# A gated graph network and a graph attention layer on one core: eight unread matrix products, a product and a spread moved in TensorE's last stage, and one subtraction moved behind a copy at the start

## The chip, the core and the metric

The kernel runs on one NeuronCore of a Trainium2 chip. Its engines are TensorE (PE in the profile; its weight loads are PEld), VectorE (DVE), ScalarE (ACT), GpSimd (POOL) and the sync engine (SP), which issues most transfers. Each engine works through its own queue in order and waits on semaphores for the others. The metric is the device time of one execution in microseconds; lower is better.

## The reference

64 graphs of 256 nodes with 256 features, an integer adjacency matrix each. Two layers, both with a layer norm and a ReLU ahead and a residual behind:

```python
# layer 0: gated graph network, 3 steps
h = relu(layernorm(x))
A = (adj != 0)
for i in range(3):
    m = h @ weight[i]
    aggr = einsum('bst,bsd->btd', A, m)
    h = gru_cell(aggr, h, w_ih, w_hh, b_ih, b_hh)
x = x + h

# layer 1: graph attention, 4 heads of 64
h = relu(layernorm(x))
f = h @ W.T + b                               # values, per head
logits = leaky_relu(f·a_src [row] + f·a_dst [column], 0.2)
logits = where(adj == 1, logits, -9e15)
out = softmax(logits) @ f
x = x + out
```

## The kernel before

The graphs are worked two at a time: 32 pairs, numbered 0 to 31, of 512 rows each. A pair passes through three recurrent steps (class `Step`, six ticks each) and then through the attention stage. Work of several pairs is interleaved: `at(tick, phase, p, fn)` puts each piece of work into a plan, and at the end the plan is read out tick by tick. What is read out is recorded in that order, and each engine gets its instructions in that order; nothing is reordered afterwards. PSUM has eight banks, in two pools: five for the gates (`gate_bank`) and three for the rest (`bank`). A new tile takes a bank of its pool when the last reader of the tile before it has finished, so the order of the work also decides who waits for a bank.

**The start.** For pair 0, `xn` is the normalised input (L368, VectorE). `first_hi` (L834, ScalarE) rounds its ReLU to the high halves `hNhi`, and `first_lo` (L838, VectorE) subtracts to get the low halves `hNlo`. At about the same place of the plan, `step_weights(0, [3])` multiplies weights on TensorE (`pc`, L243) and copies the two results to SBUF, the first on VectorE and the second on ScalarE (L247). The transposes `pt_a` (L387) and `pw_hh` (L182) follow on TensorE, in the same three banks; VectorE copies the first two `pw_hh` to `hh_T` (L183) and makes `edge` from the adjacency (L818); then the first aggregation `pa` (L493) begins. The plan has `rest(-3 if p else -6, first_lo)` for `first_lo`, `at(-6, REST, 0, ...)` for `step_weights(0, [3])`, and the biases at -5.

**The end.** For the last pair (31) `plan_tail` writes out one list, `order`, by hand, in which the rest of pairs 29 and 30 is laid between the steps of pair 31. In the code, `do(what, 2, ...)` is work of pair 29 and `do(what, 1, ...)` of pair 30. The pair's two graphs are told apart by an index 0 or 1. The steps that matter here:

- `g.difference`, `g.update` (L577, L582, L583, VectorE): the end of the last recurrent step; their result is `hT_a`.
- `turn_back` (`pback`, TensorE) transposes it back, `residual` (VectorE) adds it to `x`, `stats` and `result` (L642 to L655, VectorE, with a power on POOL, L646) normalise to `xn_b`, `turned` (`pt_b`, L664, TensorE) transposes that, with a ReLU on ScalarE (L667) to `hT_b`.
- `values` (`pv`, L673, TensorE) and `values_out` (L680, VectorE) make the values `val`.
- `spread_neighbours` (`drow`), `spread_own` and `own_and_link` (`own`), and `spread_tops` (`mrow`) spread scores over all partitions by transposes on TensorE (L688, L714, L720). `link` holds the mask as bf16 numbers, written well before.
- `maxima` (L747 to L754, VectorE) finds the row maxima `top`; `logits` and `leaky` build the logits; `exps` adds `mrow` on VectorE (L763) and takes the exponential on ScalarE (L764; for pair 30, L1040).
- `product` and `out` (`po`, L597, TensorE) multiply with the values, 16 matmul records each; `divided` divides on VectorE (`rden` L606, `o` L612) or ScalarE (L610) and adds to `x` on POOL or VectorE (L617); `write` stores to DRAM from SP's queue (L586).

The rows of pair 30's maxima are added to its logits by two transfers of 1 MB that POOL issues (`add_rows`, L986).

Of the kernel before, what the change touches and what calls it, by code (L numbers as in the profile page):

```python
# [27 lines left out]
def gated_gnn_then_gat_kernel(  # L28
# [39 lines left out]
    nc = tc.nc  # L68
# [29 lines left out]
    def bank(name):  # L98
        return ps_m.tile([P, 512], F32, tag="mm", name=name)
# [5 lines left out]
    def buf(tag, shape, name, dtype=F32):  # L105
        return sb.tile(shape, dtype, tag=tag, name=name, bufs=BUFS.get(tag, 1))
# [50 lines left out]
    ident16 = const.tile([P, P], BF16, name="ident16")  # L157
    nc.vector.tensor_copy(ident16, ident)

    def gate_bank(name):  # L160
        return ps_g.tile([P, 512], F32, tag="g", name=name)
# [460 lines left out]
    def plan_tail(t0, p, v, g, turn_back, residual):  # L622
# [15 lines left out]
        def stats(i):  # L638
            st = small.tile([P, KN, 6], F32, tag="st", name=f"st_b{p}_{i}")
            mv[i] = small.tile([P, KN, 2], F32, tag="mv", name=f"mv_b{p}_{i}")  # L640
            for s in range(KN):
                nc.vector.bn_stats(st[:, s, :], v["x"][:, i * KN + s, :])  # L642
                nc.vector.bn_aggr(mv[i][:, s, :], st[:, s, :])
            rstd[i] = small.tile([P, KN], F32, tag="rstd", name=f"rstd_b{p}_{i}")
            nc.vector.tensor_scalar_add(rstd[i], mv[i][:, :, 1], EPS)
            nc.gpsimd.tensor_tensor(rstd[i], rstd[i], mhalf[:, :KN], ALU.pow)  # L646

        def result(i):
            if i == 0:
                v["xn"] = buf("xn", [P, R, D], f"xn_b{p}")  # L650
                v["hT_b"] = buf("hT_b", [P, KD, T], f"hT_b{p}")
                v["val"] = buf("val", [P, R, VW], f"val_{p}")
                v["top"] = small.tile([P, R, H], F32, tag="top", name=f"top_{p}", bufs=2)
            for s in range(KN):
                nc.vector.tensor_scalar(  # L655
                    v["xn"][:, i * KN + s, :], v["x"][:, i * KN + s, :], mv[i][:, s, 0:1], rstd[i][:, s : s + 1],
                    op0=ALU.subtract, op1=ALU.mult,
                )

        def turned(i):  # L660
            pt = bank(f"pt_b{p}_{i}")
            for k in range(KD):
                for s in range(KN):
                    nc.tensor.transpose(  # L664
                        pt[:, k * N + s * P : k * N + (s + 1) * P], v["xn"][:, i * KN + s, ts(k, P)], ident
                    )
            nc.scalar.activation(of(v["hT_b"], i), by_c(pt), AF.Relu)  # L667

        def values(i):
            for r in range(i * KN, (i + 1) * KN):  # L670
                pv[r] = bank(f"pv_{p}_{r}")
                for k in range(KD):
                    nc.tensor.matmul(  # L673
                        pv[r][:, :VW], v["hT_b"][:, k, ts(r, P)], w_val[:, k, :],
                        start=(k == 0), stop=(k == KD - 1),
                    )

        def values_out(i):
            for r in range(i * KN, (i + 1) * KN):
                nc.vector.tensor_add(v["val"][:, r, :], pv[r][:, :VW], b_val)  # L680
# [62 lines left out]
        def maxima(i):  # L743
            for h_ in range(H):
                for r in range(i * KN, (i + 1) * KN):
                    any_ = buf("any", [P, N], f"any_{p}_{r}_{h_}")
                    nc.vector.tensor_tensor_reduce(  # L747
                        any_, two(drow[i][h_ // 2])[:, h_ % 2, :], v["noedge"][:, r, :], 1.0, -3.0e38,
                        ALU.add, ALU.max, accum_out=v["top"][:, r, h_ : h_ + 1],
                    )  # L750
            t = v["top"][:, xs[i], :]
            nc.vector.tensor_add(t, t, v["val"][:, xs[i], S0 : S0 + H])
            nc.vector.scalar_tensor_tensor(t, t, ALPHA, t, op0=ALU.mult, op1=ALU.max)
            nc.vector.tensor_scalar(t, t, barred, -1.0, op0=ALU.max, op1=ALU.mult)  # L754

        def spread_tops(i):
            mrow[i] = spread(i, "mrow", v["top"])

        def exps(i):
            for y in range(H // 2):  # L760
                for j in range(KN):
                    z_ = pairs_of_heads(i, j)[y]
                    nc.vector.tensor_add(z_, z_, two(mrow[i][y]))  # L763
                    nc.scalar.activation(z_, z_, AF.Exp)  # L764

        def out(r):
            product(p, r, zz[r // KN], v, gate_bank)

        def do(what, q, *key):
            return left[what, p - q, *key]  # L770

# [1 line left out]
        order = (  # L773
            lambda: g.difference(0), lambda: g.update(0), do("product", 2, 0), do("rows", 1), do("product", 2, 1),
            lambda: turn_back(0), lambda: g.difference(1), lambda: residual(0), lambda: stats(0), lambda: g.update(1),
            do("add", 1), do("product", 2, 2), lambda: turn_back(1), lambda: result(0), lambda: turned(0),
            lambda: residual(1), lambda: stats(1), do("product", 2, 3), do("divided", 2, 0), lambda: values(0),
            lambda: result(1), do("divided", 2, 1), lambda: turned(1), lambda: values_out(0), do("divided", 2, 2),
            do("divided", 2, 3), do("write", 2), lambda: spread_neighbours(0), lambda: own_and_link(0, 0),
            lambda: leaky(0, 0, psum=True), lambda: values(1), lambda: own_and_link(0, 1),  # L780
            lambda: leaky(0, 1, psum=True), lambda: maxima(0), lambda: values_out(1), lambda: spread_tops(0),
            lambda: spread_own(1), do("exps", 1, 0), do("product", 1, 0), lambda: exps(0),
            lambda: spread_neighbours(1), lambda: logits(1), lambda: leaky(1, 0, 1), do("divided", 1, 0),
            do("exps", 1, 1), lambda: out(0), do("product", 1, 1), lambda: out(1), do("product", 1, 2),
            lambda: maxima(1), lambda: spread_tops(1), do("product", 1, 3), lambda: exps(1),
            lambda: divided(p, 0, v, nc.gpsimd.tensor_add), do("divided", 1, 1),
            lambda: divided(p, 1, v, nc.gpsimd.tensor_add), lambda: write(p, v["x"], 0, KN), do("divided", 1, 2),
            do("divided", 1, 3), do("write", 1),
# [6 lines left out]
    def plan_pair(p):  # L795
        t0 = APART * p
        v = {}
# [9 lines left out]
        def rest(t, fn):  # L807
            at(t0 + t, REST, p, fn)
# [30 lines left out]


        ready(-3 if p else -6.5, first_hi)
        rest(-3 if p else -6, first_lo)

        def back(l, i):

# [13 lines left out]
        def turn_back(l, i):  # L859
            pt = v["pback", i] = bank(f"pback_{p}_{l}_{i}")  # L860
            for s in range(KN):
                for k in range(KD):
                    nc.tensor.transpose(  # L863
                        pt[:, s * D + k * P : s * D + (k + 1) * P], h["hT"][:, k, ts(i * KN + s, P)], ident
                    )

        def residual(i):
            xi = flat(v["x"][:, i * KN : (i + 1) * KN, :])
            nc.vector.tensor_add(xi, v["pback", i], xi)
# [43 lines left out]
        def values(r0):  # L913
            def fn():
                if r0 == 0:
                    v["val"] = buf("val", [P, R, VW], f"val_{p}")
                for r in (r0, r0 + 1):
                    pt = bank(f"pv_{p}_{r}")
                    for k in range(KD):
                        nc.tensor.matmul(  # L920
                            pt[:, :VW], hb["hT"][:, k, ts(r, P)], w_val[:, k, :],
                            start=(k == 0), stop=(k == KD - 1),
                        )
                    if dma_b:
                        nc.vector.scalar_tensor_tensor(
                            v["val"][:, r, :], pt[:, :VW], xn_b["rstd"][:, r : r + 1], b_val,
                            op0=ALU.mult, op1=ALU.add,
                        )
                    else:
                        nc.vector.tensor_add(v["val"][:, r, :], pt[:, :VW], b_val)  # L930
                if r0 == 0:
                    v["score"] = small.tile([P, R, 2 * H], F32, tag="score", name=f"score_{p}", bufs=2)
                nc.vector.tensor_copy(v["score"][:, r0 : r0 + 2, :], v["val"][:, r0 : r0 + 2, S0:])
            return fn
# [64 lines left out]
        def maxima(r, h0):  # L999
            def fn():  # L1000
                if r == 0 and h0 == 0:
                    v["top"] = small.tile([P, R, H], F32, tag="top", name=f"top_{p}", bufs=2)
                for h in (h0, h0 + 1):
                    any_ = buf("any", [P, N], f"any_{p}_{r}_{h}")
                    nc.vector.tensor_tensor_reduce(  # L1005
                        any_, drow[r // KN][:, h, :], v["noedge"][:, r, :], 1.0, -3.0e38, ALU.add, ALU.max,
                        accum_out=v["top"][:, r, h : h + 1],
                    )
            return fn
# [27 lines left out]
        def exps(i, j):  # L1037
            def fn():
                zz = logits[i][:, j, :, :]
                nc.scalar.activation(zz, zz, AF.Exp)  # L1040
            return fn
# [94 lines left out]
```

## Time and profile before

| | |
|---|---|
| median of 3 runs | 2479.35 us (2479.33 to 2479.52) |
| profiled execution | 2477.57 us, of which the span from the first to the last instruction is 2475.7 us |
| PE busy | 2454.0 us (99%) |
| DVE busy | 1983.2 us (80%) |
| ACT busy | 1442.3 us (58%) |
| POOL busy | 495.2 us (20%) |
| mean granted TensorE clock | 0.998 |

All times in the views count from the first instruction of the profiled execution. In a timeline a row is a run of like instructions: start, length, engine, line, operation, output and inputs, shape, number, and in brackets the engine's idle time ahead of it with what ended that. In a table of stretches each engine has its busy time with the number of instructions in brackets, then the granted clock of TensorE (1.00 is full), the busy share of the DMA engines and the rate. The trace's first record of the granted clock stands at 5.07 us; what lies ahead of that is shown as 1.00 for want of a record.

### The profile page before, as it was taken

The numbers are of one execution on the slowest core, as the hardware profiler recorded it, in microseconds if no ns is written. First come the engines' busy times: TensorE is split into PE (matmuls) and PEld (weight loads), VectorE is DVE, ScalarE is ACT, GpSimd is POOL, SyncE is SP. The second block draws the span as 40 slices with busy tenths as digits, with TensorE's granted clock in tenths as the row PEclk, the third lists the DMA queues.
The fourth block names the chain that finished last, engine by engine and source line by source line (L and its number), as shares of the span: only waits on it lengthen the run. The fifth ranks groups of instructions, "written<-read, shape, count | busy, mean of one in ns | idle before, by whom it ended". The sixth has DMA issues, their size and how long they took to land.

```text
span 2475.7 us, 37524 instructions
## 1 busy us (share of the span) xinstructions
PE 2454.0 (99%) x13418; PEld 2184.1 (88%) x13418; DVE 1983.2 (80%) x4659; ACT 1442.3 (58%) x3024; POOL 495.2 (20%) x422
## 2 busy tenths in 40 slices
PE   9999999999999999999999999999999999999998
PEld 7888898888898888888888988888888889888887
DVE  6678887788877888877888778888778887778777
ACT  4455556655556656556555566555565555665666
POOL 0011222112121212121221212121212212121222
PEclk9999999999999999999999999999999999999999
DMA  3026565646656555656456566557564566564455
GB/s 96 26 76 129 129 142 124 157 118 127 145 122 143 138 118 129 154 119 154 115 127 143 131 135 144 116 129 155 115 154 121 126 139 137 129 146 119 102 115 126
DMA packets 322106, 313.72 MB, mean 127 GB/s; under 512 B 166576, under 2 KB 282240, under 8 KB 321920
## 3 DMA queue, kind: packets, MB, share of 16 engines
q0 software_dynamic: 33728, 130.03, 27.8%
q1 hardware_dynamic: 286624, 181.29, 27.7%
q8 instruction: 106, 1.74, 0.3%
q14 instruction: 80, 0.66, 0.1%
q10 hardware_dynamic: 1568, 0.01, 0.0%
HBM read 215.62 MB, written 56.60 MB: 110 GB/s over the span
## 4 chain that ended last, share of the span: by engine, by line
PE 84%; DVE 12%; ACT 3%; issue 1%; DMA 0%; POOL 0%; SPq 0%; ACTq 0%; DVEq 0%; POOLq 0%
PE pd L328 18%; PE pn L328 13%; PE pc L328 10%; PE po L597 9%; PE pe L328 7%; PE pa L493 5%; PE qb L464 5%; PE p L328 5%; PE pv L920 5%; PE qa L464 4%; PE pback L863 2%; DVE hT_a L583 2%; DVE R L582 2%; DVE hNlo L854 1%; DVE any L1005 1%; ACT zz L1025 1%
## 5 line engine op out<-in xcount | busy, mean ns | idle before, releaser
L328 PE MATMUL pn<-aggr,w_a 128*128 128x256 f32 x1536 | 364.9, 380 | 2.8 <-DVE pn L549 2.8
L328 PE MATMUL pd<-T,w_a 128*128 128x256 f32 x1536 | 364.5, 380 | 0.0
L564 POOL TENSOR_TENSOR R<-hT_a,hn 128x512 f32<-128x512 f32 x95 | 140.1, 1475 | 1090.5 <-ACT hn L560 1070.7
L328 PEld LDWEIGHTS pn<-aggr,w_a 128*128 128x128 f32 x1536 | 286.8, 190 | 44.0 <-issue 2.1
L328 PEld LDWEIGHTS pd<-T,w_a 128*128 128x128 f32 x1536 | 286.9, 190 | 37.0
L597 PEld LDWEIGHTS po<-val,zz 128*128 128x128 f32 x2048 | 246.2, 193 | 5.8 <-ACT zz L1040 1.1
L560 ACT ACTIVATE hn<-pn,bi 128x256 f32<-128x256 f32 x384 | 160.8, 471 | 145.8 <-PE pn L328 145.7
L617 POOL TENSOR_TENSOR x<-x,o 128x256 f32<-128x256 f32 x126 | 137.9, 1096 | 538.9 <-DVE o L612 533.8
L582 DVE SCALAR_TENSOR_TENSOR R<-Z,R 128x512 f32<-128x512 f32 x192 | 132.5, 690 | 140.9 <-POOL R L564 126.3
L597 PE MATMUL po<-val,zz 128*128 128x65 f32 x2048 | 243.7, 273 | 0.7 <-ACT zz L1040 0.7
L1025 ACT ACTIVATE zz<-zz,val 128x256 f32<-128x256 f32 x496 | 223.8, 505 | 0.0
L1005 DVE CUSTOM_DVE_ANT_0 any<-drow,noedge 128x256 f32<-128x256 f32 x496 | 208.2, 420 | 10.6 <-DMA drow<-score_dram 1.9
L549 DVE SCALAR_TENSOR_TENSOR pn<-R,hn 128x512 f32<-128x512 f32 x192 | 149.3, 777 | 75.2 <-ACT R L471 53.5
L471 ACT ACTIVATE R<-pc,brz 128x256 f32<-128x256 f32 x192 | 80.6, 471 | 220.8 <-PE pc L328 220.8
L471 ACT ACTIVATE R<-pe,brz 128x256 f32<-128x256 f32 x192 | 80.6, 471 | 213.1 <-PE pe L328 213.1
L328 PE MATMUL pd<-T,w_h 128*128 128x256 f32 x768 | 184.4, 383 | 3.0
L328 PE MATMUL p<-T,w_a 128*128 128x256 f32 x768 | 181.6, 379 | 0.0
L328 PE MATMUL pe<-aggr,w_a 128*128 128x256 f32 x768 | 181.4, 379 | 0.0
L328 PE MATMUL pc<-aggr,w_a 128*128 128x256 f32 x768 | 181.4, 379 | 0.0
L328 PE MATMUL pc<-hT_a,w_h 128*128 128x256 f32 x768 | 181.4, 379 | 0.0
L854 DVE TENSOR_TENSOR hNlo<-pback,hNhi 128x512 fp32r<-128x512 f32 x128 | 88.3, 690 | 114.0 <-ACT hNhi L853 114.0
L328 PEld LDWEIGHTS pd<-T,w_h 128*128 128x128 f32 x768 | 143.5, 190 | 32.7 <-DVE pe L533 14.4
(190 smaller groups left out, 5307.3 us busy)
## 6 DMA issues: line engine op xcount, KB each, us to landing
zz<-score_dram POOLq DMA_DIRECT2D x62, 1024.0 KB, 11.1
zz<-topT_dram POOLq DMA_DIRECT2D x62, 1024.0 KB, 8.0
adj<-in_adj_dram SPq DMA_DIRECT2D x64, 512.0 KB
drow<-score_dram SPq DMA_DIRECT2D x62, 512.0 KB
x<-in_x_dram SPq DMA_DIRECT2D x32, 512.0 KB
out_dram<-x SPq DMA_DIRECT2D x31, 512.0 KB
words_dram_a<-words_a SPq DMA_DIRECT2D x30, 512.0 KB
words_dram_b<-words_b SPq DMA_DIRECT2D x29, 512.0 KB
```

What stands on the lines that cost most here:

```text
L328: nc.tensor.matmul(pt[:, ts(c, N)], w[:, k, j * D + c * P : j * D + (c + 1) * P], src[:, k, :], start=start and c == 0 and k == 0, stop=(c ...
L464: nc.tensor.matmul(pt, w_n[:, j, :], src, start=start, stop=True, skip_group_check=True)
L471: nc.scalar.activation(of(dst, i)[:, c, :], src[:, c, :], AF.Tanh, bias=brz[:, g0 + c : g0 + c + 1], scale=0.5)
L493: nc.tensor.matmul(pt[:, ts(i, N)], hN[half][:, i * KN + s, ts(e, P)], edge[:, i * KN + s, :], start=(s == 0 and half == 0), stop=(s == KN ...
L549: nc.vector.scalar_tensor_tensor(by_c(self.bank(f"pn{i}")), of(self.R, i), 1.0, of(self.hn, i), op0=ALU.add, op1=ALU.mult)
L560: nc.scalar.activation(n__[:, c, :], p_n[:, c, :], AF.Tanh, bias=bi[:, 2 * KD + c : 2 * KD + c + 1])
L564: nc.gpsimd.tensor_sub(of(self.R, i), of(self.hT(), i), n__)
L582: nc.vector.scalar_tensor_tensor(d_, of(self.Z, i), 1.0, d_, op0=ALU.add, op1=ALU.mult)
L597: nc.tensor.matmul(po[:, ts(h_, VC)], zz[:, j, h_, ts(s, P)], v["val"][:, i * KN + j, ts(h_, VC)], start=(j == 0), stop=(j == KN - 1),)
L617: add(v["x"][:, r, :], v["x"][:, r, :], o)
L1005: nc.vector.tensor_tensor_reduce(any_, drow[r // KN][:, h, :], v["noedge"][:, r, :], 1.0, -3.0e38, ALU.add, ALU.max, accum_out=v["top"][:, ...
L1025: nc.scalar.activation(zz[:, h, :], zz[:, h, :], AF.Prelu, alpha=ALPHA, bias=v["val"][:, r, S0 + H + h : S0 + H + h + 1],)
```

## The change

Three edits.

1. In `plan_tail`, a new function `keep` issues four matmuls of `link` (128x512, bf16) with the bf16 identity into a gate bank of its own; nobody reads the result. It stands twice in `order`: behind `turned(0)` and behind `values(0)`. Also, pair 29's fourth product, `do("product", 2, 3)`, goes from behind `stats(1)` to ahead of `turn_back(1)`.
2. In the same list, `maxima(1)` and `spread_tops(1)` go ahead of `do("product", 1, 2)`. Only `spread_tops` and the products are on TensorE's queue; VectorE's own order stays as it was, and so do those of ScalarE, POOL and SP.
3. For pair 0, `first_lo` goes from tick -6 to -5.5. On VectorE's queue the copy of `pc` (L247) then stands ahead of `hNlo` (L838); the other queues keep their order.

The function and the moved entries, cut:

```diff
+        kept = []
+
+        def keep():
+
+            if not kept:
+                kept.append(gate_bank("keep_1"))
+            for _ in range(4):
+                nc.tensor.matmul(
+                    kept[0], ident16, v["link"][:, 0, :, :].rearrange("q j n -> q (j n)"), start=True, stop=True,
+                    skip_group_check=True,
+                )
...
-            do("add", 1), do("product", 2, 2), lambda: turn_back(1), lambda: result(0), lambda: turned(0),
-            lambda: residual(1), lambda: stats(1), do("product", 2, 3), do("divided", 2, 0), lambda: values(0),
-            lambda: result(1), do("divided", 2, 1), lambda: turned(1), lambda: values_out(0), do("divided", 2, 2),
+            do("add", 1), do("product", 2, 2), do("product", 2, 3), lambda: turn_back(1), lambda: result(0),
+            lambda: turned(0), keep, lambda: residual(1), lambda: stats(1), do("divided", 2, 0), lambda: values(0),
+            keep, lambda: result(1), do("divided", 2, 1), lambda: turned(1), lambda: values_out(0), do("divided", 2, 2),
...
-            do("exps", 1, 1), lambda: out(0), do("product", 1, 1), lambda: out(1), do("product", 1, 2),
-            lambda: maxima(1), lambda: spread_tops(1), do("product", 1, 3), lambda: exps(1),
+            do("exps", 1, 1), lambda: out(0), do("product", 1, 1), lambda: out(1), lambda: maxima(1),
+            lambda: spread_tops(1), do("product", 1, 2), do("product", 1, 3), lambda: exps(1),
...
-        rest(-3 if p else -6, first_lo)
+        rest(-3 if p else -5.5, first_lo)
```

## The prediction

> **What bounds the kernel.** I read the page first, then the chain of waits, then the two ends of the run in stretches and as timelines.
>
> The page's fourth part says that the chain that ended last is TensorE's:
>
> ```profile
> PE 84%; DVE 12%; ACT 3%; issue 1%; DMA 0%; POOL 0%; SPq 0%; ACTq 0%; DVEq 0%; POOLq 0%
> ```
>
> Between 20 and 2430 us PE works nearly without a gap, and all else there is timed by PE. The change touches nothing in it, so a start that comes earlier by x moves everything behind it by x. What can be won lies in the first 20 us and the last 45 us. The end, in stretches of 2 us:
>
> ```profile
> core 0: us, PE busy (x) PEld busy (x) DVE busy (x) ACT busy (x) POOL busy (x), PEclk, DMA share, GB/s
> 2436.00:2438.00 2.00, 0.74 (x6) 0.66 (x7) 1.86 (x5) 0.97 (x3) 2.00 (x3) 1.00 0.00 0
> 2438.00:2440.00 2.00, 2.00 (x14) 2.00 (x15) 1.86 (x7) 0.60 (x1) 1.39 (x2) 0.69 0.64 115
> 2440.00:2442.00 2.00, 2.00 (x9) 1.86 (x9) 1.24 (x5) 0.93 (x4) 1.44 (x2) 0.50 1.04 207
> 2442.00:2444.00 2.00, 2.00 (x6) 1.48 (x5) 0.55 (x3) 0.93 (x4) 0.72 (x1) 0.50 1.13 156
> 2444.00:2446.00 2.00, 2.00 (x11) 1.67 (x10) 0.59 (x3) 0.19 (x1) 0.00 (x0) 0.60 0.99 166
> ```
>
> The column PEclk: the granted clock halves. Finer stretches put the fall at 2438.77 us, the return at 2445.60 and a last fall at 2472.90. The distances, 6.83 and 27.30 us, are 2 and 8 times 3.413 us, so the clock is decided on a grid of 3.413 us. PE's timeline there:
>
> ```profile
> 2433.49 1.90 PE L597 MATMUL po<-val,zz 128*128 128x65 f32 x16
> 2437.26 0.63 PE L863 MATMUL pback<-ident,hT_a 128*128 128x128 f32 x4 [1.87 <-DVE hT_a L583]
> 2437.72 0.69 PE L664 MATMUL pt_b<-ident,xn_b 128*128 128x128 f32 x4
> 2438.25 3.04 PE L597 MATMUL po<-val,zz 128*128 128x65 f32 x16
> 2441.09 3.88 PE L673 MATMUL pv<-w_val,hT_b 128*128 128x268 f32 x8
> 2444.76 1.01 PE L664 MATMUL pt_b<-ident,xn_b 128*128 128x128 f32 x4
> 2445.61 1.04 PE L688 MATMUL drow<-ident,val 128*128 128x128 f32 x8
> ```
>
> A product (po x16) takes 1.73 us elsewhere, here 2.84; the values (pv x8) take 1.81 elsewhere (2448.0), here 3.67. I count PE's work by moved columns (a po record moves 65 columns in 0.112 us, a transpose 128 in 0.109, so po counts half). The grid window 2435.36 to 2438.77 was worked 0.36 of its time, and the clock fell; 2452.42 to 2455.84 was worked 0.42, 15.31 to 18.72 (nothing but transposes) 0.54, and it did not. The line lies between 0.36 and 0.42. The halved window with 0.73 (2438.77) did not lift the clock, the one with 1.00 did.
>
> VectorE waits for this slow PE, and once more near the end:
>
> ```profile
> 2440.87 1.15 DVE L655 TENSOR_SCALAR xn_b<-x,mv_b,rstd_b 128x256 f32<-128x256 f32 x2 [0.76 <-POOL rstd_b L646]
> ...
> 2445.01 0.44 DVE L680 TENSOR_TENSOR val<-pv,b_val 128x268 f32<-128x268 f32 x1 [1.35 <-PE pv L673]
> ...
> 2464.46 2.48 DVE L763 TENSOR_TENSOR zz<-zz,mrow 128x512 f32<-128x512 f32 x4 [2.77 <-PE mrow L688]
> ```
>
> At the start PE waits 2.15 us for a PSUM bank that a weights' copy on VectorE frees, and that copy stands behind hNlo, which waits for ScalarE's hNhi:
>
> ```profile
> 14.67 1.23 DVE L838 SCALAR_TENSOR_TENSOR hNlo_a<-xn_a,hNhi_a 128x1024 fp32r<-128x1024 f32 x1 [1.12 <-ACT hNhi_a L834]
> 15.81 0.55 DVE L247 COPY w_a<-pc 128x384 f32<-128x384 f32 x1
> ...
> 17.44 1.02 DVE L183 COPY hh_T<-pw_hh 128x384 f32<-128x384 f32 x2 [0.73 <-PE pw_hh L182]
> ```
>
> **Start: the copy ahead of hNlo, -1.2 us.** Only VectorE's order changes. The copy's input ends at 12.55 (the fourth of eight pc records, 12.06 + 0.49), xn_a at 13.56, so the copy runs 13.56 to 14.11, in the 1.12 us that VectorE idled; hNlo keeps its 14.67, as hNhi ends at 14.64. PE's second pt_a goes from 16.42 to about 14.2. The pw_hh transposes then wait for banks freed by ScalarE's copies: 15.05, 15.55, 16.05, ready before VectorE is. VectorE is next to be late: hNlo to 15.81, three bias steps of some 0.15 us to 16.22, hh_T copies, edge. hh_T starts at 16.22 instead of 17.44, so edge and PE's first pa come 1.22 us earlier. Nothing in it waits for a load: SP's queue issued a descriptor at 13.0 that waits for hh_nat and the next for adj, which had to wait 1.0 us at most, so both were there by about 14.6. If the three bias steps or a bank bring less, 0.9; more than 1.4 has no room.
>
> **End: the fourth product ahead of the turn, and keep, -2.8 us.** Times are still those of before. po x16 fills 2435.22 to 2437.01 in the 1.87 us wait for hT_a, which lands as ever (2437.11): cost nothing, cover 0.2 us. pback and pt_b stay at 2437.26 to 2438.25. Then four keep products (bf16, 128x512), a shape without a row. Nearest: own<-link 128x256 bf16, x2 in 0.22 us. By columns 0.22 each, 0.86 for four; bounds are 0.44 (no dearer than 256 columns) and 1.72 (at half clock). I take 0.86, the row's own rate. Its bank was read last by hn at 2430.5, its operand link long ago: no new wait. They lie in PE's wait for hT_b (2438.45 + 0.60 = 2439.05): pv runs 2439.11 to 2440.92. The second four end at 2441.78, inside the wait for xn_b's second half (2442.02); at 1.72 they would cost 1.5 us here, at 0.44 nothing changes. pt_b ends about 2442.45; val on VectorE follows rden (2441.94) to 2442.82 and is late next. So drow starts at 2442.86 instead of 2445.61: 2.75. On the other branch ScalarE's o (to 2443.14), hT_b (2443.02 instead of 2445.81), o, own and pv give 2.79, and PE reaches mrow at 2448.3 instead of 2451.11. exps of pair 30 then starts at 2449.3; its rows landed at 2445.87 and 2451.87, the second needed at 2456.5; the output of pair 29, issued 2.8 us earlier, could delay that by its own 1.6 us, still in time. I take 2.78.
>
> With this every window holds 0.46 or more up to drow. [...]
>
> **End: spread_tops ahead of two products, -1.66 us.** drow ends at 2456.65; three products instead of four follow (64 records in 7.10 us, 1.77 each), so mrow starts 1.77 us earlier than 2463.75. top was ready at 2461.68, mrow would start at 2461.98: cover 0.3 us; without it mrow waits for top. VectorE's zz adds start 1.77 earlier, and with them rden, o and POOL's five adds of 0.68, which carried the end. Now PE is late next: it does the same work, minus its 0.23 us wait for exps, and its last result comes at 2470.09; rden, o, x of the last rows follow to 2471.29 instead of 2472.45: 1.16. The last write landed at 2474.79, 2.31 after its issue, queued behind 512 KB of pair 30 issued at 2471.12. That write is now 1.7 us earlier and gone; the 256 KB write at 2469.76 landed after 2.18, less 0.38 for half the bytes gives 1.8: 0.5 more. SP and POOL keep their orders. Bounds 0 (writes as slow) and 0.6.
>
> **Sum.** 1.22 + 2.78 + 1.16 + 0.5 = 5.66 us. The profiled execution took 2477.57 us (span 2475.7 and 1.87 around it) and would take 2471.9. The timed median is 1.78 us above it; what that is no view shows, so I carry the difference: 2479.35 - 5.66 = 2473.7; a small allowance for waits unseen, 2473.8. A change of 0.2% (4.96 us, 2474.4 to 2484.3) is about what a measurement can tell from none.
>
> **Rivals.**
> *Keep buys nothing.* If the grid lies elsewhere against the program in the timed runs, before may not lose its clock: only windows starting from 2433.05 to 2435.53 hold under 0.39, and 2435.36 is near the edge. VectorE's val at 2442.8 would bound before as well, and 2.78 goes: 2476.5. [...] Against the rival: three runs within 0.19 us, all slower than the profiled one. Also here: the clock falls in spite of keep. Chance 0.15.
> *The end is hidden.* PE or the writes end as before, or top comes late, and 1.22 + 2.78 = 4.0 us remain: 2475.3. Against: the 2.77 us wait, and POOL's chain behind it, are plain. Chance 0.10, a start that gives nothing (2474.9) in it.
> *Slower: the clock falls ahead of the last products.* The window around 2453 to 2456 holds two waits for exps; shifted by 4.0 us against the grid it becomes 2453.0 to 2456.4 with 0.46. Under about 0.4 the clock halves, and the products, moving columns half of their time, would not lift it (0.73 did not): seven products at 3.41 instead of 1.79 add 11.3 us: 2485.0. Against: no phase of that stretch holds under 0.42. Chance 0.04.
> [...]
>
> **Numbers.** Forecast 0.71, its own range 2472.9 to 2474.9; about 0.11 of that lies past 2474.4. Faster by over 0.2%: 0.60; within: 0.36 (0.11 and the two small rivals); slower 0.04. Range 2472.4 to 2476.6: the low end lets some of the 1.78 us be clock lost in the first 20 us, where windows from 12.79 to 14.52 hold under 0.39 and would go too; the high end takes in the first rival.
>
> **What would show it.** PE at clock 1.00 from 2437 to the end but for a last fall; no idle over 0.5 us before pback; drow some 4.0 us earlier than 2445.61 on the span's clock; the first pa near 18.0; DVE's L763 wait of 2.77 near 1; the last write landing 1.8 us after its issue. A clock of 0.50 anywhere before the last 3 us, or a first pa after 18.5, would make it wrong.

## The result and the profile after

The changed kernel takes 2472.79 us (median of 14 runs, 2472.04 to 2473.96), the kernel before beside it 2478.66 (14 runs, 2475.28 to 2479.99): a ratio of 0.9979, interval 0.9971 to 0.9987. That is 5.9 us, and 0.21%, at the very bound of 0.2% that the prediction set for a difference: the interval, 0.13% to 0.29%, shows a difference and leaves open on which side of that bound it lies. The profiled execution took 2472.28 us with a span of 2470.4; before it was 2477.57 and 2475.7. The runs of before fall into two groups: of all 115, 31 lie under 2477.0 us (mean 2475.93) and 84 above (mean 2479.03). The granted clock, which is on record as a mean for each of the 101 runs beside the experiments, parts them in the same place: all 27 under 2477.0 had 0.999 or 1.000, and 72 of the 74 above had 0.996 to 0.998. The upper group is thus the runs that lost more of the clock; why some do and some don't is taken up below.

The chain that ended last, on the page of after, is as it was, TensorE's:

```profile
PE 84%; DVE 12%; ACT 3%; issue 1%; DMA 1%; SPq 0%; POOL 0%; ACTq 0%; DVEq 0%; POOLq 0%
```

The same five stretches of the end, of the changed kernel:

```profile
core 0: us, PE busy (x) PEld busy (x) DVE busy (x) ACT busy (x) POOL busy (x), PEclk, DMA share, GB/s
2436.00:2438.00 2.00, 1.86 (x14) 1.44 (x15) 1.86 (x5) 0.49 (x2) 2.00 (x3) 1.00 0.00 0
2438.00:2440.00 2.00, 2.00 (x10) 1.44 (x9) 1.21 (x6) 0.91 (x5) 1.28 (x2) 1.00 1.02 193
2440.00:2442.00 2.00, 2.00 (x11) 0.97 (x9) 1.93 (x7) 0.86 (x5) 0.76 (x2) 1.00 1.17 217
2442.00:2444.00 2.00, 1.98 (x17) 1.65 (x17) 1.43 (x8) 2.00 (x10) 1.01 (x2) 1.00 0.93 106
2444.00:2446.00 2.00, 2.00 (x14) 1.73 (x12) 1.74 (x9) 1.91 (x7) 1.17 (x2) 1.00 1.04 203
```

PEclk is 1.00 in all five; it was 0.69, 0.50, 0.50 and 0.60 from 2438 on. The clock first falls at 2469.15, behind the last product. PE's timeline of the changed kernel:

```profile
2436.47 0.63 PE L875 MATMUL pback<-ident,hT_a 128*128 128x128 f32 x4
2436.93 0.70 PE L664 MATMUL pt_b<-ident,xn_b 128*128 128x128 f32 x4
2437.46 1.03 PE L776 MATMUL keep<-link,ident 128*128 128x512 bf16 x3
2438.33 2.06 PE L673 MATMUL pv<-w_val,hT_b 128*128 128x268 f32 x8
2440.22 1.03 PE L776 MATMUL keep<-link,ident 128*128 128x512 bf16 x4
2441.09 0.74 PE L664 MATMUL pt_b<-ident,xn_b 128*128 128x128 f32 x4
```

No bracket is left: the wait of 1.87 us ahead of the second pback is gone, pv x8 takes 2.06 instead of 3.88, and four keep products take 0.87 us from start to next start (2437.46 to 2438.33; one record of the first four is missing). VectorE, near the end and at the start, in the changed kernel:

```profile
13.47 0.55 DVE L247 COPY w_a<-pc 128x384 f32<-128x384 f32 x1
14.68 1.23 DVE L850 SCALAR_TENSOR_TENSOR hNlo_a<-xn_a,hNhi_a 128x1024 fp32r<-128x1024 f32 x1 [0.66 <-ACT hNhi_a L846]
...
16.16 1.01 DVE L183 COPY hh_T<-pw_hh 128x384 f32<-128x384 f32 x2
...
2420.28 0.43 DVE L1017 CUSTOM_DVE_ANT_0 any<-drow,noedge 128x256 f32<-128x256 f32 x1 [2.48 <-DMA drow<-score_dram]
...
2459.08 2.48 DVE L763 TENSOR_TENSOR zz<-zz,mrow 128x512 f32<-128x512 f32 x4 [0.99 <-PE mrow L688]
```

The copy lies in the wait for hNhi, hh_T follows with no wait, and the wait of L763 for mrow fell from 2.77 to 0.99 us. One row is worse than before, the fourth: VectorE's wait for pair 30's score rows, which before was

```profile
2421.03 0.42 DVE L1005 CUSTOM_DVE_ANT_0 any<-drow,noedge 128x256 f32<-128x256 f32 x1 [1.88 <-DMA drow<-score_dram]
```

### The profile page after: what moved, and what is told of

Its sections match the earlier page's. It is cut to its first block, busy times and chain, and to the rows that moved or that the text cites. A ratio compares the mean times of both kernels' runs of the same rounds, so it can differ in the third digit from the quotient of the medians.

```text
span 2470.4 us, 37540 instructions
## 1 busy us (share of the span) xinstructions
PE 2454.5 (99%) x13425; PEld 2183.0 (88%) x13426; DVE 1982.3 (80%) x4659; ACT 1441.0 (58%) x3024; POOL 495.5 (20%) x422
## 3 DMA queue, kind: packets, MB, share of 16 engines
q8 instruction: 106, 1.74, 0.3%
## 4 chain that ended last, share of the span: by engine, by line
PE 84%; DVE 12%; ACT 3%; issue 1%; DMA 1%; SPq 0%; POOL 0%; ACTq 0%; DVEq 0%; POOLq 0%
PE pd L328 18%; PE pn L328 13%; PE pc L328 9%; PE po L597 9%; PE pe L328 7%; PE pa L493 5%; PE qb L464 5%; PE p L328 5%; PE pv L932 5%; PE qa L464 4%; PE pback L875 2%; DVE hT_a L583 2%; DVE any L1017 2%; DVE R L582 2%; DVE hNlo L866 1%; ACT zz L1037 1%
```

## The experiments

Each kernel ran 11 times (one of them 10) beside runs of before on the same chip. The theory is the prediction's: the product's move and keep hold the clock at the turn, the tops' move takes away a wait, the copy's move brings the start forward, and the three add up. The first rival is its "keep buys nothing", with the clock's grid elsewhere in other runs.

**The product's move alone.** Before, with one edit:

```diff
-            do("add", 1), do("product", 2, 2), lambda: turn_back(1),
-            lambda: residual(1), lambda: stats(1), do("product", 2, 3), do("divided", 2, 0),
+            do("add", 1), do("product", 2, 2), do("product", 2, 3), lambda: turn_back(1),
+            lambda: residual(1), lambda: stats(1), do("divided", 2, 0),
```

> The kernel before with nothing but pair 29's fourth product moved ahead of the turn. Grid: no fall of the clock in the last 40 us whatever the phase of the grid; drow about 6.2 us after the last hT_a instead of 9.2; median about 2476 to 2477 (2475.7, the fast group of before, plus up to 1.7 in the half of the runs in which the clock falls in the first 20 us). Rival 'keep holds the clock': as before, 2478.7.

Measured: 2475.49 us (2475.01 to 2476.57), ratio 0.9991 (0.9982 to 1.0). The upper group is gone: no run is above 2476.6, and the mean, 2475.58, is that of before's lower group (2475.93) or a little less. The clock of the profiled run is 1.00 from 5.86 us to 2470.28. Its PE timeline at the turn:

```profile
2434.40 3.69 PE L597 MATMUL po<-val,zz 128*128 128x65 f32 x32
2438.17 0.63 PE L863 MATMUL pback<-ident,hT_a 128*128 128x128 f32 x4
...
2440.01 2.08 PE L673 MATMUL pv<-w_val,hT_b 128*128 128x268 f32 x8 [0.69 <-ACT hT_b L667]
```

Without keep PE still waits, 0.69 us here and 0.60 in all ahead of pt_b's second half, and that costs no clock. So the move of one product, with no work added, removes the loss.

**The keep products alone.** Before, with `keep` at its two places and the fourth product where it was:

```diff
-            lambda: turn_back(1), lambda: result(0), lambda: turned(0),
+            lambda: turn_back(1), lambda: result(0), lambda: turned(0), keep,
...
-            do("product", 2, 3), do("divided", 2, 0), lambda: values(0),
+            do("product", 2, 3), do("divided", 2, 0), lambda: values(0), keep,
```

> The kernel before with the two sets of four keep products at their places and nothing else: the wait of 1.87 us ahead of the turn stays. The keep products come behind that wait. Theory A (counted windows): windows that end before the first keep are as little worked as ever, those that reach past it gain up to 0.25: the phases that lose the clock shrink from 73% to about 50%, and a lost clock is lifted one window earlier, since the keep products fill the next one. So still two groups: some 4 to 6 of 11 runs at 2475.5 to 2476.5, the others at 2477 to 2479, median about 2477. Theory B (keep is what holds the clock): all runs within 2475.2 to 2476.7, no fall of the clock in the profiled run before the last 4 us. Theory C (keep is for nothing here, and its PE time is in the way): as the kernel before or up to 1 us slower, median 2478.5 to 2479.5.

Measured: 2478.15 us (2476.07 to 2480.33), ratio 0.9999 (0.999 to 1.0008); one run of 11 lies under 2477. Theory B is out. In the times, A's shift to more runs in the lower group did not show, nor did C's extra time. The mean granted clock says something more: five of the ten runs above 2477 had 0.999, as only 2 of the 74 such runs of before had. So by this mean keep alone did shorten the loss of clock in some runs, as A foresaw, but no time was won by it; what took the gain back (keep's own 0.87 us ahead of needed work, at each of its places, is one candidate) no run here shows. The profiled run, at 2479.97:

```profile
2437.94 0.63 PE L875 MATMUL pback<-ident,hT_a 128*128 128x128 f32 x4 [1.87 <-DVE hT_a L583]
2438.41 0.69 PE L664 MATMUL pt_b<-ident,xn_b 128*128 128x128 f32 x4
2438.94 1.54 PE L776 MATMUL keep<-link,ident 128*128 128x512 bf16 x4
```

The wait of 1.87 us stands as before, keep comes behind it, and the clock falls at 2439.31 in the middle of keep (1.54 us instead of 1.03) and returns at 2446.14, 6.83 us or two windows later, as in before. Of the work put behind the wait, 0.37 us of keep still fell into the window that holds the wait (2435.89 to 2439.31, PE busy for 1.55 of its 3.42 us), and the clock fell all the same.

**The changed kernel without keep.**

```diff
-            lambda: turned(0), keep, lambda: residual(1), lambda: stats(1), do("divided", 2, 0), lambda: values(0),
-            keep, lambda: result(1),
+            lambda: turned(0), lambda: residual(1), lambda: stats(1), do("divided", 2, 0), lambda: values(0),
+            lambda: result(1),
```

> The changed kernel without its two keep calls; the rest of the change stays. Theory 'grid': the clock falls only if a grid window of 3.413 us is worked less than some 0.36 to 0.42 by TensorE, counted by columns; with the product moved no window of the last 40 us is under 0.43 even without keep (counted on the trace of the changed kernel with the keep records struck out). So the clock stays at 1.00 to the end of TensorE's work, drow starts about 6.15 us after the last hT_a (as in the changed kernel) and the time is that of the changed kernel, 2472.8, within 0.3. Rival 'keep holds the clock': without keep the clock falls between 2435 and 2442, drow starts 8.5 us or more after hT_a, and the time is 2475.0 to 2476.

Measured: 2473.14 us, ratio 0.9983 (0.9974 to 0.9992). Ten runs lie from 2471.54 to 2474.13, as the changed kernel's, so keep costs nothing and gives nothing there that these runs resolve. The eleventh, which was the profiled one, took 2479.72. Its stretches, cut at the times of its clock's changes and every 3.41 us between them, show where:

```profile
2429.59:2433.00 3.41, 2.56 (x24) 2.43 (x24) 3.10 (x13) 3.41 (x10) 0.00 (x0) 1.00 0.94 187
2433.00:2436.42 3.42, 3.42 (x19) 3.42 (x18) 2.51 (x6) 2.00 (x6) 0.00 (x0) 0.50 0.07 14
...
2443.24:2446.66 3.42, 2.73 (x8) 1.92 (x7) 2.52 (x9) 1.52 (x5) 0.91 (x2) 0.50 1.12 164
2446.66:2450.07 3.41, 3.41 (x13) 2.81 (x12) 1.69 (x6) 1.42 (x6) 1.26 (x2) 0.50 1.00 197
2450.07:2453.48 3.41, 3.41 (x26) 3.12 (x25) 2.83 (x13) 3.20 (x13) 1.46 (x2) 1.00 0.62 124
```

The clock fell at 2433.00 and stayed at 0.50 to 2450.07, 17.07 us or five windows. VectorE's timeline and PE's of the same run show what was late:

```profile
2427.53 0.43 DVE L1017 CUSTOM_DVE_ANT_0 any<-drow,noedge 128x256 f32<-128x256 f32 x1 [0.87 <-DMA drow<-score_dram]
```

```profile
2431.98 0.28 PE L955 MATMUL ptopT<-ident,top 128*16 128x128 f32 x1 [0.85 <-DVE top L1028]
```

The second half of pair 30's score rows landed late, PE's transpose of the tops waited for VectorE, and the window before 2433.00, else filled with products, held 0.38 by the prediction's count. This is ahead of keep's first place (2437.46 in the changed kernel). Whether keep would have shortened the five windows this run cannot tell. The profiled runs of two other kernels below lost the clock behind such late rows too.

**The tops' move alone, and the changed kernel without it.** The first is before with the second edit of the change, the second is the changed kernel with that edit taken back:

```diff
-            lambda: out(1), lambda: maxima(1), lambda: spread_tops(1), do("product", 1, 2), do("product", 1, 3),
+            lambda: out(1), do("product", 1, 2), lambda: maxima(1), lambda: spread_tops(1), do("product", 1, 3),
```

> The kernel before with nothing but maxima(1) and spread_tops(1) ahead of product(1,2). Forecast of the prediction: the second L763 starts 1.77 us earlier against drow, the last x add 1.16, the last landing 1.66; TensorE's end hardly moves. Time 1.66 us under before in each phase: median about 2477. Rival 'the end is hidden': TensorE or the writes end as before, under 0.5 us.

Measured: 2477.26 us, from 2473.47 to 2481.02, ratio 0.9994 (0.9985 to 1.0003). The runs of this kernel, which lost the clock in some of them and not in others, spread by 7.5 us, and 1.7 us can't be read from 11 of them. The profiled run is the slowest, and the moved entries, which come later, are not the reason: the second half of pair 30's score rows came 1.13 us late there, PE's ptopT waited 1.22 us, and the clock was 0.50 from 2433.85 to 2450.92, 17.07 us as in the run without keep. It shows a loss at the start too. Its stretches there:

```profile
13.80:17.21 3.41, 1.48 (x12) 1.13 (x11) 2.00 (x5) 1.80 (x4) 0.00 (x0) 1.00 1.10 349
17.21:20.62 3.41, 3.35 (x16) 2.93 (x15) 2.99 (x6) 2.16 (x7) 1.19 (x2) 0.50 0.27 44
```

PE was busy for 1.48 us of the 3.41 up to 17.21, and the clock was 0.50 from there to 20.62. The last of the eight pa on hNhi started at 22.17, against 21.37 in before with the same start of xn_a (12.18 and 12.17): 0.8 us.

> The changed kernel with the second tops spread behind the third product again, as before the change. Its runs have no loss of clock at the end to hide the step (14 runs of the changed kernel from 2472.0 to 2474.0 us, mean 2472.8). Theory: the step is worth 1.2 us by the last rows and 0.5 us by a last write that isn't queued, at any clock: mean 2474.5 us, within 0.5; in the trace L763 (DVE) waits about 2.8 us for PE's mrow, and the last write lands about 2.3 us after its issue. Rival: the last rows are bound by PE's products whatever the order: mean under 2473.3, L763's wait moved elsewhere.

Measured: 2474.89 us, ratio 0.9987 (0.9978 to 0.9996); ten runs from 2473.99 to 2475.36 with a mean of 2474.72, and one at 2478.50. All 25 runs of the changed kernel (below) have a mean of 2473.07, so the step is worth 1.65 us. VectorE's timeline of this kernel has the old wait again:

```profile
14.88 0.56 DVE L247 COPY w_a<-pc 128x384 f32<-128x384 f32 x1 [1.36 <-PE pc L243]
...
2461.93 2.48 DVE L763 TENSOR_TENSOR zz<-zz,mrow 128x512 f32<-128x512 f32 x4 [2.77 <-PE mrow L688]
```

The upper row shows the start under another phase of the grid: the clock rose first at 11.44 us here (8.14 in the changed kernel's profile), pc was late (its second half began at 13.29 us, against 11.63), the copy waited 1.36 us for it and hNlo (15.36, against 14.68) came behind the copy. edge came at 18.32, hardly earlier than before's 18.38.

**The copy's move alone, and the changed kernel without it.** One edit each way, `rest(-3 if p else -6, first_lo)` against -5.5.

> The kernel before with nothing but first_lo at -5.5. Both theories: the first pa 1.28 us earlier than 19.21, at 17.9. Grid adds: the window of little work from 12.8 to 16.2 is gone, so the runs of before that lost clock there (phases of 1.74 in 3.41 us) win about 1.5 us more; the end still loses its clock for 2.5 of 3.4 us of phases. Two groups, about 2474.4 and 2477.2; median about 2477. Rival 'plain shift': all runs 1.3 us faster than before, spread as wide as that of before.

Measured: 2478.58 us, ratio 0.9998 (0.9989 to 1.0007); three runs at 2474.26 to 2474.54 and eight from 2477.81 to 2479.88. The two groups stay, as the end is untouched. The lower three lie 1.5 us under before's lower group, the upper eight (mean 2478.82) only 0.2 under its upper one and 1.6 above the 2477.2 that was expected. So few runs don't size the step, and why the upper group hardly moved stays open.

The profiled run (2474.47) is one of the lower three, and it shows how a kernel with the old end escapes the loss. The wait is there, and the clock stays at 1.00 up to 2469.88. Steps of 3.413 us, counted back from there, cut the turn so:

```profile
2436.96 0.63 PE L863 MATMUL pback<-ident,hT_a 128*128 128x128 f32 x4 [1.87 <-DVE hT_a L583]
```

```profile
2432.33:2435.74 3.41, 2.56 (x22) 2.31 (x21) 3.25 (x10) 2.96 (x8) 0.09 (x1) 1.00 0.03 5
2435.74:2439.15 3.41, 2.19 (x20) 2.11 (x20) 3.20 (x8) 1.55 (x4) 3.35 (x3) 1.00 0.20 19
```

pback is 0.30 us earlier than in before, so by the prediction's count the windows that hold under 0.39 start from 2432.75 to 2435.23 here. These two start just outside: the wait is shared between them, and each holds more (0.39 and 0.45 by the count given below) than the windows that a fall followed (0.32 to 0.37).

> The changed kernel with the weights' copy behind hNlo again. Theory: from the end of hNhi to the first pa 1.29 us more, so 2474.1 us, within 0.5. Windows that start between 12.9 and 14.9 us hold under 0.39 of work here, so about half the runs should lose the clock for one window near 17 to 20 us and be longer by the delay of the transposes there, some 0.3 to 0.8 us: a spread up to 2475, without a second group 3 us higher. Rival: the copy's place is hidden by loads that come late, and the runs lie at 2472.8 like those of the changed kernel.

Measured: 2474.12 us (2473.45 to 2475.43), mean 2474.27, ratio 0.9984 (0.9975 to 0.9992): 1.2 us above the changed kernel's 2473.07. The time from the start of xn_a to that of edge on VectorE, over all profiled runs, sizes it better:

| | xn_a to edge, us |
|---|---|
| copy behind hNlo, clock up by 5.9 us in three, at 10.52 us in the last | 6.21, 6.21, 6.22, 6.22 |
| copy behind hNlo, where the clock fell at 17.21 | 6.48 |
| copy ahead of hNlo, clock up by 8.2 us | 4.91, 4.92, 4.92 |
| copy ahead of hNlo, clock up at 10.42 and 11.44 us | 5.63, 6.18 |

The step is worth 1.30 us, 0.59 where the clock comes up at 10.42 us, and next to nothing (0.03) where it comes up at 11.44; the old order was traced with a rise at 10.52 us, but with none as late as 11.44.

**A version with the bias steps ahead as well.** `first_lo` goes on to tick -4.9, so that VectorE's three bias steps (L191 to L193) also fall into the wait for hNhi. It was run in three forms: with pair 30's ptopT behind the next product (the second part of the diff) and without keep; with keep; and without keep.

```diff
-        rest(-3 if p else -5.5, first_lo)
+        rest(-3 if p else -4.9, first_lo)
...
-            do("product", 2, 0), do("rows", 1), do("product", 2, 1),
+            do("product", 2, 0), do("product", 2, 1), do("rows", 1),
```

> The changed kernel without keep, with VectorE's three bias steps ahead of hNlo too (they lie in its 0.66 us wait for hNhi), and with the transpose of pair 30's tops on PE (ptopT) behind the second product of pair 29's first half instead of ahead of it. Theory: the bias steps bring the first pa 0.35 to 0.4 us earlier (hh_T follows hNlo at once); the ptopT step costs and brings nothing in a usual run (0 to 0.2 us) and takes away PE's wait in runs whose score rows land late, the only place where the changed kernel without keep has lost its clock (1 run of 11): mean 2472.3 us, no run over 2474.5. Rival: the tops' rows, sent some 1.7 us later, reach ScalarE's exps too late: 2473.5 to 2474.5.

Measured: 2472.88 us, ratio 0.9982 (0.9973 to 0.9991); nine runs from 2472.02 to 2473.99 (mean 2472.78), two at 2478.19 and 2478.71. The later tops cost nothing, but runs that lose the clock stay, and the traced one of them again had late rows: in it (2478.19) VectorE waits 0.98 us for the rows, PE's wait has only gone from ptopT to the turn, and the clock is 0.50 from 2433.51 to 2447.16:

```profile
2433.88 1.09 PE L875 MATMUL pback<-ident,hT_a 128*128 128x128 f32 x4 [1.21 <-DVE hT_a L583]
```

hT_a stands behind the same maxima on VectorE's queue. The idea was wrong in that step.

> The changed kernel once more, beside the version above: 2472.0 to 2474.0 us, median 2472.7. If keep holds the clock where rows land late, no run is over 2474.5; if it does nothing there, one run in some 20 is near 2478 to 2480, as in the kernel without it (1 of 11) and in the one with the old order of tops, which has keep (2478.50, 1 of 11).

Measured: 2473.23 us (2472.95 to 2474.16), ratio 0.9982 (0.9973 to 0.999). With the first 14 runs that makes 25 of the changed kernel, mean 2473.07, none above 2474.2.

> The changed kernel with VectorE's three bias steps ahead of hNlo too; keep and everything else as in the changed kernel. Theory: 0.41 us less between hNlo and hh_T where PE's pw_hh transposes are ready by then (clock up by about 8 us), about 0.3 us where the first clock rise comes after 10 us: mean 2472.4 to 2472.7 us against 2473.1 for the 25 runs of the changed kernel so far. Rival: hh_T waits for pw_hh either way, and the mean is 2473.1 or more.

Measured: 2472.70 us (2471.54 to 2474.34, 10 runs), ratio 0.9977 (0.9968 to 0.9986).

> The same without the keep products. If keep does nothing, the usual runs lie where those with keep lie, within 0.3 us in the mean, and 0 to 2 of 11 runs are near 2478 to 2480 here as there. If keep costs PE time, 0.3 to 0.9 us less; if keep is what holds the clock when rows land late, more such runs here than with it (so far 3 of 33 runs with the product moved and no keep, 1 of 47 with it).

Measured: 2472.78 us (2471.79 to 2473.76), ratio 0.9977 (0.9968 to 0.9986). The two means, 2472.86 and 2472.90, are 0.2 us under the changed kernel's; with runs that spread by 0.6 us (one standard deviation) that is not resolved. xn_a to edge is 4.58 with an early clock, 0.33 less than 4.91, but 5.42 and 5.45 where the clock came up after 10 us. Keep makes no difference in the usual runs (0.04 us, with a standard error of 0.3). Over all kernels that have the product moved, the clock was lost, by the run's time and its mean granted clock of 0.996 or 0.997, in 1 of 57 runs with keep and in 3 of 44 without. By chance alone three or all of such four runs would fall on the side without keep in about 2 of 10 cases, so a use of keep against late rows is neither shown nor excluded.

## Why the prediction was right

The time lies 1.0 us under the forecast of 2473.8: inside the range of 2472.4 to 2476.6, 0.1 us below the forecast's own of 2472.9 to 2474.9. The mechanism was the one named, the product moved into the wait; keep, named beside it, turned out to have no part in the time won. Of the 1.0 us, 0.7 is the base: the forecast started from three runs of before that all were of the upper group (2479.35), and its median beside the changed kernel was 2478.66. Between the two medians 5.87 us were won, where 5.66 were summed up. By its steps, on the profiled executions:

- **Start, -1.22:** 1.29. The first pa went from 19.21 to 17.92 (foreseen: near 18.0), with the copy in VectorE's wait. What the prediction left out is that pc itself can be late: with the clock up at 10.42 us less than half is won, and at 11.44 us nothing.
- **Product and keep, -2.78:** 2.80 from hT_a to the first L763 (hT_a 0.79 earlier, L763 3.59 earlier, 2451.80 to 2448.21). The price taken for four keep products, 0.86 us, came out at 0.87. But the term belongs to the product's move alone. Neither keep alone nor keep on top of the move changed the time.
- **Tops, -1.66:** mrow came 1.79 us further forward (1.77 foreseen), L763's wait ended at 0.99 (foreseen near 1), the last addition to x came 1.16 earlier on top of the 3.59 (1.16 foreseen), and the last write landed 1.74 us after its issue (1.8 foreseen). With the write's 0.57 that is 1.73; 1.65 by the timed runs.
- **Not foreseen, +0.50:** the start's 1.29 had shrunk to 0.79 at hT_a, because VectorE waited 2.48 us instead of 1.88 for pair 30's score rows. In the other profiled runs this wait is between 2.17 and 2.93, whatever the kernel; it belongs to the run, not to the change.

1.29 + 2.80 + 1.16 + 0.57 - 0.50 = 5.32, the difference of the spans (5.3). Predicted were 5.66.

The term that was mis-sized is the 1.78 us between the profiled execution and the median, which the prediction carried over whole. After the change 0.51 were left (2472.79 less 2472.28; 0.79 by the mean of 25 runs). No run shows the whole of it. Part of it was clock lost in the first 20 us, worth 0.8 us in the one run whose trace shows it; the windows from 12.79 to 14.52 that held under 0.39 by the prediction's count are gone once the copy is ahead. Another part may be the wait for the score rows, which the profiled run of before had at 1.88, the shortest of thirteen. The low end of the range had allowed for this.

The first rival's premise was true, and its chance of 0.15 rested on a weak argument. Before does escape the loss in some of its runs, in the way that the trace of the copy alone shows. The prediction's own trace gave the share: 2.48 us of window starts out of 3.413 hold under 0.39, 73%, and 84 of the 115 runs, 73%, lie in the upper group (between 70% and 79%, as the cut is moved over the ten runs between 2476.3 and 2477.6). Three runs of the upper group in a row, which the prediction took as evidence against a moving grid, happen with 0.73 x 0.73 x 0.73 = 0.39. In the escaped runs the rival's sum holds: without the 2.78, 1.22 + 1.16 + 0.5 = 2.88 us are left to win, and the changed kernel's mean (2473.07) lies 2.86 under that of the lower group. So the 2.78 is won in some three runs of four, and over all runs the means differ by 5.1 us (2478.19 and 2473.07). That the upper group is as large as the share is not a clean test, since some of its runs may have lost the clock by late rows instead.

That the clock is decided on a grid of 3.413 us was drawn from 6.83 and 27.30 us, which are also 1 and 4 times 6.83. The trace of before has a third distance: 2433.70 us from the first record of the clock (5.07; the four transposes from 3.95 us, ahead of it, take 0.213 each as at clock 0.50) to the fall at 2438.77 are 713 steps of 3.4133, but 356.5 of 6.83. In the changed kernel the 2461.01 us from 8.14 to 2469.15 are 721 such steps, and in the tops' move alone the clock was low for one step, from 17.21 to 20.62. Against the program the grid moves from run to run: the first rise lies between 4.71 and 11.44 us in thirteen profiled runs, at places that are not whole windows apart (5.07, 6.12 and 6.97 in three of them).

Neither the length of a gap nor PE's busy time told which windows lost the clock: in the run without keep the largest gap of the window that lost it was 0.85 us, and PE was busy for 2.56 of its 3.41 us, while the copy alone kept the clock over a wait of 1.87 us, with PE busy for 2.56 and 2.19 us of its two windows.

What fits the falls seen here is the share of the window by moved columns. Counted in one way over all thirteen profiled runs (at full clock 128 columns of f32 count as 0.109 us and 512 of bf16 as 0.215, as eight transposes and four keep products take 0.87 us each in the changed kernel; at 0.50 both count double, as four transposes take 0.85 us in the run without keep), the windows at full clock that were followed by a fall while PE still had work held 0.32 to 0.37. The lowest that kept the clock held 0.37 (the bias steps with keep) and 0.39 (the copy alone). It is an estimate from these traces, and with 0.37 on both sides it gives no sharp line. The prediction's counts come out a little lower this way: 0.34 for its 0.36, 0.40 for its 0.42, 0.51 for its 0.54, and 0.63 for the halved window that it put at 0.73. Their order, on which its argument rests, stays.

## What to carry to other kernels

The changes of the clock lay on a grid of 3.413 us here, which moved from run to run, so that one profile showed one phase. Where traces show that, count the work in every possible window, read off what share of them holds less than the windows that a fall was seen to follow, and expect the timed runs to be a mixture in that proportion (here 73% by the count, and 84 of 115 runs). What held the clock here was to close the wait with work that is needed anyway and stands ahead of it in the queue (2475.49 us with the product's move alone, no run above 2476.6); unread work behind the wait won no time (2478.15 us). And size a small step in a kernel whose clock is already steady (the changed kernel with that step undone): the runs mostly spread by 1 to 3 us there, and by 4 to 8 where the clock is lost in some runs.

## What the hardware showed beyond that

In the run without keep the clock, once lost, stayed at 0.50 for five windows (17.07 us), with PE busy for the whole of four of them. By the count of moved columns given above the first four, at 0.50, held 0.65, 0.52, 0.68 and 0.70 and left it low; behind the fifth, full of pv and transposes, it was 1.00 again. Over all falls traced, the clock stayed low behind halved windows with 0.52 to 0.71 and rose behind those with 0.86 and more. The run took 2479.72 us, and the other ten of its kernel 2472.96 in the mean: over 6 us went with one wait of 0.87 us for a transfer. Such late rows stand in four of the thirteen profiled runs; waits of 0.87, 0.98 and 1.13 us were followed by a fall, one of 0.18 us (the bias steps without keep) was not. The start has the same lever in reverse: with the first rise at 11.44 us instead of 8.14, all but 0.03 of the 1.30 us of the copy's move were gone (6.18 us from xn_a to edge instead of 4.91, where the old order has 6.21).
